# Graph-layer stack: the roots of two quarters on GpSimd, a first stage without side checks, and a fixed order at the start of layer 2

## The chip, the cores and the metric

One core of one Trainium2 chip. The metric is the device time of one execution in microseconds (us), as the median of several runs. The engines are named PE (TensorE; PEld are its weight loads), DVE (VectorE), ACT (ScalarE), POOL (GpSimd) and SP (SyncE, which here only issues DMAs).

## The reference, cut to what matters

Four graph layers stand one behind the other, each as `x = x + layer(relu(layernorm(x)))`, on 4096 nodes of 64 values and a dense 4096 x 4096 adjacency of zeros and ones.

```
# layer 1
adj_att = sigmoid(left[:, None] + right[None, :] + b) * adj
x_local = logmap(x[:, None, :], x[None, :, :], c)       # for every pair of nodes
support = einsum('ij,ijd->id', adj_att, x_local)
out = proj(expmap(x, support, c), c)                    # norms: square roots, one tanh
# layer 2
deg = adj.sum(1) + 1
z = concat([X, (adj @ X + X) / deg]) @ W + b
out = relu(z) / max(norm(relu(z)), 1e-12)
# layer 3
rank = cumsum(adj != 0, axis=1); deg = rank[:, -1:]; k = minimum(deg, 100)
pos = rank - (deg - k)
w = (adj != 0) * where(pos > 0, 0.5 ** (k - pos), 0)
out = w @ (x @ weight) + bias
```

Layer 0 is a graph attention of eight heads with an output attention; the change doesn't touch it.

## The kernel before, in words

**Layer 1, pairs** (`pairs_fast`, L2282, 1188 to 1672 us). The 4096 nodes are 8 groups of 512, and a job is a pair of groups (gi, gj). There are 36: (0,0), (1,1), then the rows gi = 7 down to 2, each with gj = 0 to gi, and last (1,0). A job off the diagonal works both ways: node i's sum over j and node j's over i. The loop over jobs (n from -2 on, L2491) is a software pipeline of depth four: `later` is the job whose distances are worked, `soon` the one that gets its scores, `now` the one whose sums are taken, `done` the one that is closed. Each job has four steps s. In one step the code issues, in this order: the scores (`score_pair`: PE L2331 and L2337 into the two buffers pl, then ACT's sigmoid L2342 into sg), the columns of results (`last_column` and `bring` on DVE, into VT, L2443 to L2451), transposes (`turn`: PE L2387, DVE L2390), sums (PE L2397 into accj and acci), distances (PE L2351 and L2352, ACT L2353) and their squares (ACT L2363), then `end_nodes`, the factor (DVE L2371), checks of the adjacency, and the weighing of the scores (DVE L2378). `in_order` (L933) ties each instruction on PE, DVE and ACT to the one before it on its engine, so those three run in the order in which the code stands. POOL and SP are not tied.

**Ends of nodes.** When a quarter of the nodes (16 blocks of 128) has all its sums, a generator `nodes` (L3051) ends it: `finish_steps` (L2513) turns the sums into the layer's output, `norm_steps` (L994) does layer 2's layernorm, and two copies L3057 and L3064 with a difference hs (L3060) make the two fp16 halves HH of layer 2's input. The pair jobs call it through `end_nodes`: a step of the generator ends at a `yield`, and a yield of True ends the turn. Quarters 24, 16 and 8 (named by their first block) are begun in the pair jobs, as groups 6, 4 and 2 finish; quarter 0, and what is left of 8, is done by the interleaving loop at L2674 to L2680, at the start of layer 2. Each quarter needs three sets of roots of 128 x 8 values: of the norm (un, L2569), of the clip (pp, L2596), of the variance (L1020). Each has two forms, chosen by `beside[0]`: ACT's Sqrt, or `inverse_root` (L981), an estimate on DVE and three Newton rounds of four operations on GpSimd:

```
for _ in range(3):
    nc.gpsimd.tensor_tensor(t, y, y, ALU.mult)
    nc.gpsimd.tensor_tensor(t, t, v, ALU.mult)
    nc.gpsimd.tensor_scalar(t, t, -0.5, 1.5, ALU.mult, ALU.add)
    nc.gpsimd.tensor_tensor(y, y, t, ALU.mult)
```

In this kernel `beside[0]` becomes False at n = -2, before any quarter ends, so all roots are ACT's. Sigmoid and Sqrt are in different function tables of ACT.

**Checks.** All through the kernel the adjacency is read in pieces of 512 KB (`check_rows`, L967: an SP DMA at L964, four pieces ahead, and a pass on DVE, L972) to find values other than 0 and 1. `CHECKS_2` and `CHECKS_3` say how many are left for layers 2 and 3.

**Layer 2** (`layers_fast`, L2622, from 1672). Its weights come by GpSimd DMAs; L2654 works on w2e, and L2660 and L2661 fill sel, the selector for counts. The edges come in eight quarters q = 7 to 0 of 1 MB (tile m2, L2787, three buffers; SP). For each, 16 matmuls sum neighbours (nacc, L2824) and 16 count them (dc, L2834), for the first four groups of targets. hT2 is a transposed copy of the layer's input with a row of ones (a DMA at L2723). Each group's tail (`layer2_group`) then runs beside a segment: `segment(k)` (L2860) does the sums and counts of one of the four other groups of targets, sums at L2870 and counts at L2879, blocks 0 to 31 in rising order. This stage isn't in `in_order`; the framework's scheduler places its instructions.

**Layer 3** (1795 on) ranks the neighbours on PE (L2929, L2937), clamps on ACT and DVE (L2951, L2953) and sums (L2961). The weight squares wsq (L2707) feed its first small matmul pm (L2709).

Of the kernel before, what the change touches and what calls it, by code (L numbers as in the profile page):

```python
# [10 lines left out]
F32 = mybir.dt.float32  # L11
BF16 = mybir.dt.bfloat16
F16 = mybir.dt.float16
F8 = mybir.dt.float8e4
# [3 lines left out]
U8 = mybir.dt.uint8  # L18
# [41 lines left out]
NS = HW // G  # L60
QB = NB // 4
CW = N // 4
CHECKS_2 = 10
CHECKS_3 = 40
HB = NB // 2
EDGE = 56.0
EDGES4 = 0x38383838
# [774 lines left out]
def kernel(  # L842
# [235 lines left out]
    with ExitStack() as l0:  # L1078
# [1203 lines left out]
    def pairs_fast(es, VT, nodes):  # L2282
# [24 lines left out]
        with ExitStack() as ss:  # L2307
# [155 lines left out]

            def end_nodes(s, most):
                while ends and most:
                    if s % 2 == 0 and ends[0][1] < 2:
                        return
                    wait = next(ends[0][0], None)
                    ends[0][1] += 1
                    if wait is None:  # L2470
                        ends.pop(0)
                    most = 0 if wait else most - 1
# [5 lines left out]
            with in_order():  # L2478
                for n in range(-2, len(jobs) + 1):
                    done, now, soon, later = (job(n + k) for k in range(-1, 3))  # L2480
                    if later and n + 2 > 0:
                        load_edges(*later)
                    for s in range(4):
                        if soon and s // 2 < len(ways(*soon)):
                            score_pair(*ways(*soon)[s // 2], s % 2 * 2)
                        if s == 0 and done:
                            last_column(*done, 2)
                            bring(*done)
                        if s % 2 == 0 and now and now[0] != now[1]:
                            turn(*now, s)  # L2490
                        if s % 2 and now:  # L2491
                            sums(*now, s - 1)
                        if s == 2 and now:
                            last_column(*now, 0)
                        if later:
                            distance(*later, s)
                            if s % 2:
                                square(*later, s - 1)
                        busy = bool(ends)
                        beside[0] = beside[0] and bool(soon)  # L2500
                        if now:
                            end_nodes(s, 3 if not soon else 1 + s % 2 * (now[0] < 4) if s else 0)
                        if s == 1 and soon:
                            factor(*soon)
                        if n >= 0 and soon and s % 2 == 0:
                            check_edges(1 if busy else 2 if s or now[0] == now[1] else 1)
                        if s == 3 and soon:
                            weigh(*soon)
                            check_edges(4 if n < 0 else 0)
# [112 lines left out]
    VBITS = 128.0  # L2622


    def layers_fast(es, wide, nodes, ends, parts, ready):
        HO2 = N // 4
        NK = HO2 // G
        HH, SS = parts
# [45 lines left out]
        with in_order():  # L2674
            for quarter, after in zip(ends, ends[1:] + [iter(())]):
                most = 12
                for wait in quarter:
                    for _ in range(min(2, most) if wait else 0):
                        next(after, None)
                        most -= 1  # L2680

# [37 lines left out]
        late, late_x = (lp.tile([P, 2, G], BF16, name=n) for n in ("late", "late_x"))  # L2719

        valued = []
        hT2 = lp.tile([D + 1, N], F32, name="hT2")
        nc.sync.dma_start(hT2[D : D + 1, :], ones[0:NB, :])  # L2723
        for b0 in reversed(range(0, NB, GB)):
            transpose_to(
# [58 lines left out]
            nc.gpsimd.tensor_tensor(xg, xg, b3t.unsqueeze(1).to_broadcast([P, GB, D]), ALU.add)  # L2784

        def rows_of_edges(width):
            m = work.tile([P, JT * HW], U8, name="m2", tag="m2", bufs=3)  # L2787
            return m.rearrange("p (t i) -> p t i", i=width)

        def in_turn(one, other):  # L2790
# [23 lines left out]
        segments = []  # L2814
        accs = [rank_bank("nacc") for _ in range(NS)]
        dc = sum_bank("dc")
        for n, q in enumerate(reversed(range(NQ))):
            m = rows_of_edges(HW)
            nc.sync.dma_start(m, mask_d[q][0])
            m8 = m.bitcast(F8)  # L2820
            for t in range(JT):
                j = q * JT + t
                for k in range(NS):
                    nc.tensor.matmul(  # L2824
                        accs[k],
                        lhsT=HH[:, j].rearrange("p s d -> p (s d)"),
                        rhs=m8[:, t, k * G : (k + 1) * G],
                        start=(n == 0 and t == 0),
                        stop=(n == NQ - 1 and t == JT - 1),
                    )  # L2830
            for t in range(JT):
                j = q * JT + t
                for k in range(NS):
                    nc.tensor.matmul(  # L2834
                        dc[k * O : (k + 1) * O, :],
                        lhsT=sel[:, j * O : (j + 1) * O],
                        rhs=m8[:, t, k * G : (k + 1) * G],
                        start=(n == 0 and t == 0),
                        stop=(n == NQ - 1 and t == JT - 1),
                    )  # L2840
# [17 lines left out]
        in_turn_all(*(layer2_group(g * GB, ev[g], deg[:, g, :]) for g in range(NS)))  # L2858

        def segment(k):  # L2860
            acc, dc = sum_bank("nacc"), rank_bank("dc")
            m8 = [rows_of_edges(G).bitcast(F8) for _ in range(2)]
            for q in range(NQ):
                t = q * JT % HB
                nc.sync.dma_start(
                    m8[q * JT // HB][:, t : t + JT],
                    mask_d[q][1][:, :, k * G : (k + 1) * G].bitcast(F8),
                )
            for j in range(NB):
                nc.tensor.matmul(  # L2870
                    acc,
                    lhsT=HH[:, j].rearrange("p s d -> p (s d)"),
                    rhs=m8[j // HB][:, j % HB],
                    start=(j == 0),
                    stop=(j == NB - 1),
                )
            for j in range(NB):
                r = j % NS
                nc.tensor.matmul(  # L2879
                    dc[r * O : (r + 1) * O, :],  # L2880
                    lhsT=sel[:, j * O : (j + 1) * O],
                    rhs=m8[j // HB][:, j % HB],
                    start=(j < NS),
                    stop=(j >= NB - NS),
                )
            cf = work.tile([P, G], F32, name="cf", tag="cf")
            nc.vector.tensor_copy(cf, dc)
# [134 lines left out]
    with tc.If(general == 0):  # L3022
        with ExitStack() as es:
# [105 lines left out]
```

## Time and profile before

| what | value |
|---|---|
| median of 3 runs | 1965.71 us (1964.72 to 1967.07) |
| the profiled execution | 1964.7 us, span 1963.0 us |
| granted TensorE clock, mean | 0.95 |
| PE busy | 1772.9 us, 90% of the span |
| DVE busy | 1595.1 us, 81% |
| ACT busy | 1436.7 us, 73% |
| POOL busy | 85.5 us, 4%, 126 instructions |
| HBM read and written | 245.37 MB and 49.46 MB |

The span is the time from the first to the last instruction in the trace; the execution's own time has 1.7 us more. A row of the profile such as "L2342 ACT ... sg<-pl,rb" is a line of the code, its engine, what it writes and what it reads. A wait "PE pl L2331 <- ACT sg L2342" means that PE's instruction on line 2331 stood idle until ACT's on line 2342 was done. On ACT the pair stage has these table loads, by the line at which they stand (count, then busy us and mean ns, then idle us before):

```profile
L2342 ACT ACT_TABLE_LOAD x5 | 6.4, 1283 | 0.1
L2569 ACT ACT_TABLE_LOAD x3 | 3.8, 1283 | 0.1
L2596 ACT ACT_TABLE_LOAD x2 | 2.6, 1283 | 0.0
L1020 ACT ACT_TABLE_LOAD x2 | 2.6, 1283 | 0.0
```

### The profile page before, as it was taken

The numbers are of one execution on the slowest core, as the hardware profiler recorded it, in microseconds if no ns is written. First come the engines' busy times: TensorE is split into PE (matmuls) and PEld (weight loads), VectorE is DVE, ScalarE is ACT, GpSimd is POOL, SyncE is SP. The second block draws the span as 40 slices with busy tenths as digits, with TensorE's granted clock in tenths as the row PEclk, the third lists the DMA queues.
The fourth block names the chain that finished last, engine by engine and source line by source line (L and its number), as shares of the span: only waits on it lengthen the run. The fifth ranks groups of instructions, "written<-read, shape, count | busy, mean of one in ns | idle before, by whom it ended". The sixth has DMA issues, their size and how long they took to land.

```text
span 1963.0 us, 44619 instructions
## 1 busy us (share of the span) xinstructions
PE 1772.9 (90%) x19352; PEld 819.6 (42%) x19367; DVE 1595.1 (81%) x2468; ACT 1436.7 (73%) x1477; POOL 85.5 (4%) x126
## 2 busy tenths in 40 slices
PE   5889999999999989998499967999999998899998
PEld 3444444444444445454244442333333332355433
DVE  6769999998779988997768868898888676755687
ACT  3769888899768988996589956777787785323575
POOL 2000100100000000000111100000000000100000
PEclk8899999999999999998699986999999999898999
DMA  8956664425311111102265516455533110664396
GB/s 112 181 126 104 104 99 72 140 104 211 114 50 51 50 50 56 56 2 71 80 186 180 186 54 206 155 177 166 172 108 122 39 33 6 243 210 129 101 338 228
DMA packets 145962, 239.09 MB, mean 122 GB/s; under 512 B 16646, under 2 KB 106070, under 8 KB 140214
## 3 DMA queue, kind: packets, MB, share of 16 engines
q1 hardware_dynamic: 131228, 194.02, 29.7%
q0 software_dynamic: 14528, 42.13, 12.4%
q8 instruction: 153, 2.51, 0.5%
q14 instruction: 53, 0.43, 0.1%
HBM read 245.37 MB, written 49.46 MB: 150 GB/s over the span
## 4 chain that ended last, share of the span: by engine, by line
PE 51%; DVE 20%; ACT 16%; issue 6%; DMA 3%; POOL 0%; SPq 0%; DVEq 0%; ACTq 0%; POOLq 0%
ACT st L1242 9%; PE accj L2397 8%; DVE B L1248 7%; PE accC L1578 6%; PE accB L1578 3%; PE acco L2185 3%; PE pv L2937 3%; DVE st L1236 3%; PE sacc L2961 3%; PE pf L2387 2%; PE pl L2331 2%; PE accD L1578 2%; PE pu L2351 2%; PE pl L2337 2%; PE accL L1578 2%
## 5 line engine op out<-in xcount | busy, mean ns | idle before, releaser
L1242 ACT ACTIVATE st<-srow,nt 128x2048 int8<-128x2048 f32 x352 | 682.9, 1994 | 87.6 <-DVE B L1248 86.4
L1248 DVE TENSOR_TENSOR B<-st,mres 128x1024 int32<-128x1024 int32 x256 | 311.8, 1221 | 63.9 <-PE accC L1578 36.6
L1578 PE MATMUL accB<-B,ybh 128*32 128x512 fp8e4 x3072 | 255.8, 382 | 20.4 <-DVE B L1248 20.2
L1578 PEld LDWEIGHTS <-ybh 128*32 128x32 bf16 (+1 forms) x6656 | 178.5, 97 | 212.3 <-issue 57.0
L1578 PE MATMUL accC<-mres,ych 128*32 128x512 fp8e4 x2272 | 227.3, 380 | 0.0
L1578 PE MATMUL accC<-B,ycn 128*32 128x512 fp8e4 x2272 | 227.1, 379 | 0.0
L1578 PE MATMUL accD<-B,ybh 128*32 128x512 fp8e4 x2048 | 206.6, 382 | 2.1 <-DVE h L1710 2.1
L1236 DVE TENSOR_SCALAR st<-srow,nt 128x2048 uint8<-128x2048 f32 x160 | 205.4, 1285 | 1.8
L2397 PE MATMUL accj<-sg,who 128*64 128x512 f32 (+1 forms) x512 | 199.9, 621 | 7.4 <-DVE sg L2390 6.0
L2397 PE MATMUL acci<-sg,who 128*64 128x512 f32 (+1 forms) x512 | 200.6, 622 | 0.3 <-DVE VT L2451 0.3
L2353 ACT ACTIVATE yt<-pu,consts 128x512 f32<-128x512 f32 x144 | 98.6, 687 | 99.0 <-PE pu L2352 98.8
L2342 ACT ACTIVATE sg<-pl,rb 128x512 f32<-128x512 f32 x256 | 161.0, 679 | 10.9 <-PE pl L2337 8.3
L1578 PEld LDWEIGHTS <-ych 128*32 128x32 f16 x4096 | 117.7, 97 | 116.5 <-issue 12.0
L1578 PE MATMUL accL<-B,ybh 128*32 128x512 fp8e4 x1536 | 156.9, 384 | 4.1 <-DVE h L1709 4.0
L972 DVE SCALAR_TENSOR_TENSOR raw<-raw 128x1024 f32<-128x1024 f32 x128 | 153.9, 1217 | 1.5 <-DMA raw<-in_adj_dram 1.5
L1242 ACT ACTIVATE st<-srowo,nto 128x1024 int8<-128x1024 f32 x128 | 138.1, 1137 | 16.1 <-DVE B L1248 13.7
L1256 DVE TENSOR_TENSOR C<-B,mres 128x1024 int32<-128x1024 int32 x114 | 139.6, 1225 | 3.1
L1578 PE MATMUL accC<-C,ych 128*32 128x512 fp8e4 x1824 | 125.5, 385 | 6.2 <-DVE C L1256 6.1
L2951 ACT ACTIVATE w3b<-pv 128x512 int16<-128x512 f32 x168 | 89.0, 596 | 55.8 <-issue 21.2
L2331 PE MATMUL pl<-nm,noid 128*128 128x512 fp8e4 x256 | 84.2, 394 | 25.5 <-ACT sg L2342 24.4
L1578 PEld LDWEIGHTS <-ycn 128*32 128x32 f16 x2272 | 65.9, 97 | 59.6 <-issue 0.4
L2371 DVE SCALAR_TENSOR_TENSOR yt<-sqy,yt 128x1024 f32<-128x1024 f32 x72 | 84.9, 1219 | 3.4 <-ACT sqy L2363 3.4
(519 smaller groups left out, 2717.6 us busy)
## 6 DMA issues: line engine op xcount, KB each, us to landing
raw<-in_adj_dram SPq DMA_DIRECT2D x128, 512.0 KB, 5.0
mo<-edges SPq DMA_DIRECT2D x32, 512.0 KB, 4.3
noedge<-nmo POOLq DMA_DIRECT2D x32, 512.0 KB, 3.9
nm<-noedge SPq DMA_DIRECT2D x64, 256.0 KB, 3.0
m<-edges SPq DMA_DIRECT2D x32, 512.0 KB, 5.6
srow<-srow_d SPq DMA_DIRECT2D x15, 1024.0 KB, 7.5
mres<-in_adj_dram POOLq DMA_DIRECT2D x8, 1024.0 KB, 36.4
edges<-in_adj_dram POOLq DMA_DIRECT2D x8, 1024.0 KB, 15.0
```

The source lines that it names most:

```text
L972: nc.vector.scalar_tensor_tensor(raw, raw, 0.0, raw, ALU.is_gt, ALU.not_equal, accum_out=bad[:, c : c + 1])
L1236: nc.vector.tensor_scalar(st[:, i, :].bitcast(U8), srow, negs[:, i : i + 1], EDGE, ALU.is_gt, ALU.mult)
L1242: nc.scalar.activation(st[:, i, :], srow, AF.Sign, bias=negs[:, i : i + 1], scale=-1.0)
L1248: nc.vector.tensor_tensor(B.bitcast(I32), st.bitcast(I32), edges.bitcast(I32), ALU.bitwise_and)
L1256: nc.vector.tensor_tensor(C.bitcast(I32), B.bitcast(I32), edges.bitcast(I32), ALU.bitwise_xor)
L1578: ins = nc.tensor.matmul(acc[k * O : (k + 1) * O, :], lhsT=values, rhs=moving(k), start=start, stop=stop,)
L2331: nc.tensor.matmul(pl, lhsT=noid, rhs=nm[:, b, :].bitcast(F8), start=True, stop=False)
L2342: nc.scalar.activation(sg[:, b0 + k, :], pl, AF.Sigmoid, bias=rb[:, j : j + 1], scale=1.0)
L2353: nc.scalar.activation(far[gi, gj][:, b, :], pu, AF.Sigmoid, bias=nb_t, scale=2.0 * DIST_K / (DIST_S * DIST_S),)
L2371: nc.vector.scalar_tensor_tensor(y, squares.pop((gi, gj, b0)), F_K1, y, ALU.add, ALU.mult)
L2397: nc.tensor.matmul(acc[r : r + n, :], lhsT=XQ[:, src, cols], rhs=w, start=start, stop=stop)
L2951: nc.scalar.activation(wk, pvs[i, k], AF.Relu)
```

## The change

1. `CHECKS_2` goes from 10 to 12 and `CHECKS_3` from 40 to 44, and the checks that stood in the first two jobs (n = 0 and 1) are left out; the four ahead of them stay.
2. `beside[0]` is True for all jobs but the last, so the roots of quarters 24 and 16 are made by `inverse_root`; those of 8 and 0 still by ACT. `end_nodes` waits for an odd step only while `beside[0]` is True, and the last job takes up to four steps of ends at a time rather than three.
3. hT2 is no tile of its own: it lies in VT, which is free once the last fold matmuls have read it. m2 has five buffers in place of three.
4. In the loop that ends the last quarters, the next quarter moves one step at each wait rather than two.
5. The main sums of layer 2 are put in program order, two quarters at a time: q = 7, 6 and 5, 4 with sums and counts each; then the counts of 3 and 2, the sums of the first segment over its second half of blocks (16 matmuls), the sums of 3 and 2; then the counts and the sums of 1 and 0. Segments run over falling blocks, their second half first.

GpSimd loads its function library once. In the instruction order of before this stands ahead of L2654; in that of the changed kernel it stands behind L2292, at the start of the pair stage, since the first GpSimd arithmetic now comes there.

```
-CHECKS_2 = 10
-CHECKS_3 = 40
+CHECKS_2 = 12
+CHECKS_3 = 44
...
             def end_nodes(s, most):
                 while ends and most:
-                    if s % 2 == 0 and ends[0][1] < 2:
+                    if beside[0] and s % 2 == 0 and ends[0][1] < 2:
                         return
...
-                        beside[0] = beside[0] and bool(soon)
+                        beside[0] = n < len(jobs) - 1
                         if now:
-                            end_nodes(s, 3 if not soon else 1 + s % 2 * (now[0] < 4) if s else 0)
+                            end_nodes(s, 4 if not soon else 1 + s % 2 * (now[0] < 4) if s else 0)
                         if s == 1 and soon:
                             factor(*soon)
-                        if n >= 0 and soon and s % 2 == 0:
+                        if n > 1 and soon and s % 2 == 0:
                             check_edges(1 if busy else 2 if s or now[0] == now[1] else 1)
...
-                    for _ in range(min(2, most) if wait else 0):
+                    for _ in range(min(1, most) if wait else 0):
...
-        hT2 = lp.tile([D + 1, N], F32, name="hT2")
+        hT2 = VT[0 : D + 1]
...
-            m = work.tile([P, JT * HW], U8, name="m2", tag="m2", bufs=3)
+            m = work.tile([P, JT * HW], U8, name="m2", tag="m2", bufs=5)
...
-        for n, q in enumerate(reversed(range(NQ))):
+        quarters = list(reversed(range(NQ)))
...
+        def segment_sums(k, part):
+            if part:
+                acc = sum_bank("nacc")
+                halves_of[k] = acc, [None, None]
+            acc, m8 = halves_of[k]
+            m8[part] = rows_of_edges(G).bitcast(F8)
+            for q in reversed(range(part * NQ // 2, (part + 1) * NQ // 2)):
+                t = q * JT % HB
+                nc.sync.dma_start(
+                    m8[part][:, t : t + JT],
+                    mask_d[q][1][:, :, k * G : (k + 1) * G].bitcast(F8),
+                )
+            for j in reversed(range(part * HB, (part + 1) * HB)):
+                nc.tensor.matmul(
+                    acc,
+                    lhsT=HH[:, j].rearrange("p s d -> p (s d)"),
+                    rhs=m8[part][:, j % HB],
+                    start=(j == NB - 1),
+                    stop=(j == 0),
+                )
+
+        halves_of = {}
+        with in_order():
+            for n in range(0, NQ, 2):
+                two = [edges_of(q) for q in quarters[n : n + 2]]
+                if n == NQ // 2:
+                    for q, m8 in two:
+                        counts_of(q, m8)
+                    segment_sums(0, 1)
+                    for q, m8 in two:
+                        sums_of(q, m8)
+                elif n > NQ // 2:
+                    for q, m8 in two:
+                        counts_of(q, m8)
+                    for q, m8 in two:
+                        sums_of(q, m8)
+                else:
+                    for q, m8 in two:
+                        sums_of(q, m8)
+                        counts_of(q, m8)
...
         def segment(k):
...
+            if k not in halves_of:
+                segment_sums(k, 1)
+            segment_sums(k, 0)
+            acc, m8 = halves_of.pop(k)
+            dc = rank_bank("dc")
...
-            layers_fast(es, wide, nodes, ends, (HH, SS), ready)
+            layers_fast(es, wide, nodes, ends, (HH, SS), ready, VT)
```

`edges_of` loads a quarter; `sums_of` and `counts_of` hold the two loops of matmuls that stood in the old loop.

More of the change, by code (lines that the diff above doesn't have):

```diff
@@ L2622, with layers_fast @@
     VBITS = 128.0
-    def layers_fast(es, wide, nodes, ends, parts, ready):
+    def layers_fast(es, wide, nodes, ends, parts, ready, VT):
         HO2 = N // 4
@@ L2816, in layers_fast, with edges_of, sums_of @@
         dc = sum_bank("dc")
-        for n, q in enumerate(reversed(range(NQ))):
+        quarters = list(reversed(range(NQ)))
+        def edges_of(q):
             m = rows_of_edges(HW)
             nc.sync.dma_start(m, mask_d[q][0])
-            m8 = m.bitcast(F8)
+            return q, m.bitcast(F8)
+        def sums_of(q, m8):
             for t in range(JT):
@@ L2827, in layers_fast, with counts_of @@
                         rhs=m8[:, t, k * G : (k + 1) * G],
-                        start=(n == 0 and t == 0),
-                        stop=(n == NQ - 1 and t == JT - 1),
+                        start=(j == NB - JT),
+                        stop=(j == JT - 1),
                     )
+        def counts_of(q, m8):
             for t in range(JT):
@@ L2837, in layers_fast @@
                         rhs=m8[:, t, k * G : (k + 1) * G],
-                        start=(n == 0 and t == 0),
-                        stop=(n == NQ - 1 and t == JT - 1),
-                    )
+                        start=(j == NB - JT),
+                        stop=(j == JT - 1),
+                    )
+        def segment_sums(k, part):
[37 more added lines that the diff above has]
+                        counts_of(q, m8)
         cf = work.tile([P, G], F32, name="cf", tag="cf")
@@ L2860, in segment @@
         def segment(k):
[L2861 to L2877, printed above, removed]
+            if k not in halves_of:
[3 more added lines that the diff above has]
+            dc = rank_bank("dc")
+            for j in reversed(range(NB)):
                 r = j % NS
@@ L2882, in segment @@
                     rhs=m8[j // HB][:, j % HB],
-                    start=(j < NS),
-                    stop=(j >= NB - NS),
+                    start=(j >= NB - NS),
+                    stop=(j < NS),
                 )
```

## The prediction

> **What bounds the kernel now.** I read the busy time of each engine by stretch first, then what TensorE (PE) waits for there, then ScalarE's (ACT's) timeline at those waits, and last the start of layer 2. "x" counts instructions, PEclk is the granted TensorE clock.
>
> ```profile
> core 0: us, PE busy (x) PEld busy (x) DVE busy (x) ACT busy (x) POOL busy (x), PEclk, DMA share, GB/s
> 1440.00:1510.00 70.00, 61.88 (x329) 20.74 (x322) 61.74 (x108) 56.65 (x80) 0.00 (x0) 0.98 0.35 109
> 1570.00:1640.00 70.00, 62.98 (x330) 22.14 (x330) 51.81 (x90) 55.58 (x78) 0.00 (x0) 0.95 0.09 27
> 1240.00:1440.00 200.00, 194.60 (x1071) 69.62 (x1070) 173.74 (x235) 149.85 (x212) 0.00 (x0) 0.98 0.52 166
> 1672.00:1690.00 18.00, 10.90 (x47) 4.82 (x46) 15.15 (x51) 5.54 (x11) 3.04 (x7) 0.62 0.63 224
> 1690.00:1728.00 38.00, 38.00 (x258) 16.41 (x257) 20.09 (x58) 9.93 (x19) 0.00 (x0) 0.96 0.79 270
> 1630.00:1640.00 10.00, 9.57 (x42) 2.96 (x43) 4.05 (x7) 6.82 (x12) 0.00 (x0) 0.83 0.00 0
> ```
>
> Where only pairs run (1240 to 1440) PE is busy for 97% and sets the pace. In the two stretches in which a quarter of the nodes ends beside the pairs (rows 2 and 3) it is busy for 88 and 90%, though VectorE (DVE) and ACT have time left: something serial stops it. At 1630 the clock is 0.83. At the start of layer 2 (1672 to 1690) PE works 10.9 of 18 us at 0.62.
>
> PE's waits name the cause. These are the answers for 1440 to 1515, for 1585 to 1640, for 1240 to 1440, and for 1660 to 1820 (us in total, times, longest):
>
> ```profile
> PE pl L2331 <- ACT sg L2342: 8.0, 10, 2.4
> ...
> PE pl L2331 <- ACT sg L2342: 6.0, 9, 2.3
> ...
> PE pl L2331 <- ACT sg L2342: 3.8, 8, 1.2
> ...
> PE dc L2834 <- POOL sel L2661: 6.7, 1, 6.7
> ```
>
> The scores' buffers wait for ACT's sigmoids: 8.0 and 6.0 us in the quarters' stretches, against 3.8 in 200 us of plain pairs. ACT's timeline shows why, and GpSimd's (POOL's) shows the last wait:
>
> ```profile
> 1454.80 1.28 ACT L2569 ACT_TABLE_LOAD   x1
> 1456.10 0.21 ACT L2569 ACTIVATE un<-un 128x8 f32<-128x8 f32 x1
> 1456.32 1.28 ACT L2342 ACT_TABLE_LOAD   x1
> 1457.62 1.27 ACT L2342 ACTIVATE sg<-pl,rb 128x512 f32<-128x512 f32 x2
> ...
> 1686.27 0.86 POOL L2654 TENSOR_SCALAR w2e<-w2e 64x64 f32<-64x64 f32 x2 [12.50 <-issue]
> ...
> 1743.22 0.73 DVE L1023 SCALAR_TENSOR_TENSOR h<-h,ln_var 128x256 f32<-128x256 f32 x1
> 1744.07 0.42 DVE L1023 SCALAR_TENSOR_TENSOR h<-h,ln_var 128x256 f32<-128x256 f32 x1
> ```
>
> A root of eight columns (0.21 us) costs two table loads, and the next scores stand behind them. The chain of waits runs through these loads. In layer 2 the first GpSimd arithmetic (L2654) starts 12.5 us after the instruction before it; the chain has a weight's DMA until 1678.30 and then 7.97 us of "issue". The fill of sel stands behind it, and PE's counts (dc) behind that.
>
> **A. First jobs without checks.** The first two jobs lose 8 checks of 1.22 us on DVE (L972). What PE loses to them is little: it waits 1.2 us (accj for VT L2443) and 0.3 (acci for VT L2451), and works cold behind that (the first acci pair takes 1.94 us where later ones take 1.25, and 1222.7 to 1225.5 runs at half clock, some 1.35 us lost). 1.2 + 0.3 + 0.7 + 1.35 = 3.5 us. Ends: 1 (the waits only move to the first loads of nm) and 6 (the other waits of that stretch, 2.6 for the sigmoids, shrink too). Six of the eight go elsewhere: two to layer 2, four to layer 3 (the constants); costed there.
>
> **B. Roots on GpSimd.** Only the quarters that end beside jobs before the last change, 24 and 16; quarters 8 and 0 keep ACT's roots. By the order of instructions ACT loses 12 loads there: 12 x 1.283 = 15.4 us. PE gets less: its waits in the two stretches, 8.0 + 6.0, minus what row ends cost anyway (3.8 in a stretch with two of them), 10.2 us; and at 1630 to 1640 the clock of 0.83 would be 1.0, 1.7 us. Together 11.9.
>
> The rule: the Trainium skill, "ScalarE: Activation LUTs", section "What ACT_TABLE_LOAD costs", puts a switch at 1283 ns and a drain of about 1380, 2.66 us in all; 12 x 2.66 = 31.9 us would go. In the trace the next activation starts 0.02 us after the load: no drain of that size is left between them. I take the row, 15.4, as the ceiling.
>
> The new work: inverse_root is 12 dependent GpSimd operations of 128x8; with what stands around it the norm (un) has 14, the clip (pp) 12, the layernorm (ln) 13, so 39 for a quarter and 78 in all. None is in this trace. The nearest row, the pair at L2654, takes 0.86 us for two, 0.43 each: un 6.0 us, pp 5.2, ln 5.6. The generator gives them time: two pair jobs' transposes lie 12.84 us apart in the chain, so one of a job's four steps is 3.2; un is asked for after three steps (9.6), pp after two (6.4), ln after three. All fit, pp with 1.2 us to spare. If they don't, ACT's tanh (L2567) or DVE's L2606 or L1023 waits, and behind it, in program order, the next sigmoids on ACT, or on DVE the next copies of transposes and products; PE then stands for the difference. The first GpSimd arithmetic of the stage may pay its start: now it is at 1188, right behind two memsets, and unused for 250 us, so I take +1 for the first operation (0 to +8, the 7.97 of issue above).
>
> The rule against this change: the Trainium skill, "SBUF — State Buffer", section "Who interferes with whom", says GpSimd and DVE share a port pair under an exclusive lock. The rows of L1023 show it: of two equal operations in a row, the one beside GpSimd work takes 0.73 us, the next 0.42. That is 0.31 late (one at 1783.56 reads 0.96, 0.54 late). By the row at its worst the 78 operations put 78 x 0.31 = 24 us, or 78 x 0.54 = 42 us, on DVE. But DVE stood 8.3 + 18.2 = 26.5 us idle in the two stretches, of which 11.9 go if they shrink by that: 14.5 us stay to take it up[...]. I take 0.1 each, 8 us, under the slack, and +1.5 on the path. B: -11.9 + 1 + 1.5 = -9.5 us (ends -13 and -1).
>
> The last job gets four steps of ends rather than three: fold matmuls move ahead of its sums, where PE now waits 1.99 us for a product of DVE. Half of that, 1 us, is in C's sum.
>
> **C. Start of layer 2.** As GpSimd's start is paid at 1188, w2e is worked when its DMA lands: 1678.30 + 0.86 + 0.24 gives sel at 1679.4, before PE asks (1680.8). The wait of 6.7 goes, with the cold work behind it (dc 1.90 for 16 where later ones take 1.05, nacc 5.60 against 3.63: 2.9 us). Not all of it is won. In the fixed order the next matmul that must wait is layer 3's pm (L2709), for wsq on DVE, which stands behind the last quarter's end (hs at 1701.14, LDf's 2.29 us, wsq at 1705.62). The quarters' ends go one at a time instead of two, so this comes no earlier; PE, now 9.6 us ahead, would wait there about 3 us and redo some cold. Main sums end at 1725.2 instead of 1728.0: -2.8. The first segment's half, 16 matmuls, 3.6 us, only moves from behind the groups into the quarters; it fills part of the wait above, and at the end of layer 2 its absence takes 3.1 us off (4.8 us of sums there now, 1.7 then). The stretch between is bound by the groups' chain (PE waits 3.0 us there for ln_var, in three waits), and two more checks (L972) stand in it: +1.2. With the 1 us of the last job the sum is -2.8 - 3.1 + 1.2 - 1 = -5.7; I take -4.5, since the filler helps only if the chain it hides is short. Ends -10 and 0.
>
> **D. At nothing.** Four more checks in layer 3 (DVE 1.22 each, 4.9 us): PE is busy 155.5 of the last 168 us and DVE's clamps share with ACT; uncovered it costs up to 4.9. On SP's queue the ones row now lies in VT and waits for VT's last reader (about 1674.7); the quarters' loads of 1 MB behind it land about 1681, needed from 1686; two more buffers cover that. Uncovered: 3 us.
>
> **Sum.** -3.5 - 9.5 - 4.5 = -17.5. The profiled execution took 1964.7 us (span 1963.0 and 1.7 around it): 1947.2. It lies 1.0 under the median, so 1948. Its own range, half way from each term to its ends: -9.8 to -23.3, 1942 to 1956.
>
> **Rivals.**
> *R1, the waits are replaced.* pp has only 1.2 us to spare; if GpSimd operations take 0.6 us in place, DVE waits at L2606 and the scores wait for products instead of sigmoids; in layer 2 pm takes the place of sel. For it: DVE is busy 61.7 of 70 us in the first stretch. Against: the next GpSimd row is 0.43. Then A -1.5, B -4, C -1: 1965.7 - 6.5 = 1959.
> *R2, slower: the port.* Each of the 78 operations holds DVE up for p; from p = (14.5 + 11.9 + 8) / 78 = 0.44 us the slack, B's gain and the 8 us of A and C are spent. At the highest row, 0.54, it is 42 - 14.5 - 11.9 = 15.7 for B, minus 8: 1973. For it: the rows of L1023, and DVE is nearly full in the first stretch. Against: the second stretch has 18 us of room, and 0.54 was one of the longest delays.
> *R3, nothing comes of it:* PE's time is pairs, and the clock takes back what the waits gave: 1965.
>
> **Chances.** About 0.2% (4 us) is what a measurement of this kernel can tell from no change. Likeliest 0.55, all faster. R1 0.23, of which 0.05 within. R2 0.15, slower. R3 0.07, of which 0.06 within and 0.01 slower. Faster 0.73, same 0.11, slower 0.16. The range reaches from A, B and C all at their best (-6 - 13 - 10: 1937) over R1 to R3 with a little above it, 1967; R2 is left out.
>
> **What would show it.** In the changed profile: no table load on ACT from 1240 to the last job, or B has not happened. PE's wait pl for sg in the quarters' stretches at 4 us rather than 6 to 8. GpSimd rows of 0.3 to 0.45 us start to start, and no wait of DVE L2606 or ACT L2567 for POOL beyond 1 us; if these show 2 us and more, R1. DVE's mean of L2371, L2378 and L972 in those stretches up by 0.1 us at most; up by 0.3, R2. No wait of dc for sel, and instead pm for wsq near 3 us. In the first jobs accj no longer waits for VT. I am wrong if DVE is busy 95% in the quarters' stretches, or if the main sums' end isn't earlier against the last job's end.

## The result, and the profile after

The changed kernel takes 1936.96 us (median of 4 runs, 1936.5 to 1941.29) against 1966.39 for the kernel before on the same chip (4 runs): ratio 0.9855, 95% interval 0.9838 to 0.9872, 29.4 us less. Run once more, on another chip, it gave 1940.08 against 1964.41: 0.9879, 0.9864 to 0.9893, 24.3 us less. The forecast was 17.5 us faster, range 1937 to 1967. The sign is right, the size too small: the first median lies on the range's low edge, where A, B and C were all to come out at their best.

The profiled execution of the changed kernel is the slowest of its first four (1941.29, span 1939.6), 23.4 us shorter than before's. Its busy time by stretch, for the stages shown of before (the first quarter's end, the second's, plain pairs, the start of layer 2 and its main sums):

```profile
core 0: us, PE busy (x) PEld busy (x) DVE busy (x) ACT busy (x) POOL busy (x), PEclk, DMA share, GB/s
1430.00:1500.00 70.00, 67.05 (x360) 22.91 (x358) 64.73 (x111) 52.31 (x76) 12.32 (x26) 0.98 0.39 121
1555.00:1620.00 65.00, 61.51 (x340) 22.51 (x342) 51.80 (x88) 48.31 (x71) 11.18 (x27) 1.00 0.11 33
1240.00:1430.00 190.00, 184.65 (x1018) 66.00 (x1016) 166.30 (x225) 142.97 (x203) 0.00 (x0) 0.99 0.52 167
1653.00:1670.00 17.00, 16.33 (x104) 6.45 (x104) 13.99 (x43) 4.73 (x9) 3.38 (x6) 0.91 1.00 366
1670.00:1706.00 36.00, 31.03 (x212) 15.59 (x210) 19.90 (x57) 9.30 (x17) 0.61 (x1) 0.95 0.77 248
```

PE now works 96 and 95% of the quarters' stretches, close to the 97% of plain pairs. At the start of layer 2 it works 16.3 of 17 us, but the main sums behind it, which were without a gap, have one of 5 us. The waits, for 1430 to 1500, 1555 to 1622, 1645 to 1775 (PE) and 1420 to 1640 (DVE), say the same:

```profile
PE pl L2331 <- ACT sg L2342: 1.9, 4, 1.2
...
PE pl L2331 <- ACT sg L2342: 2.1, 5, 1.2
...
PE pm L2709 <- DVE wsq L2707: 5.0, 1, 5.0
...
PE dc L2840 <- POOL sel L2661: 0.3, 1, 0.3
...
DVE mden L2606 <- POOL pp_root L991: 2.7, 2, 1.5
```

8.0 and 6.0 us of waiting for sigmoids became 1.9 and 2.1; no table load is left on ACT from 1240 to 1645, where quarter 8's begin. sel's 6.7 became 0.3, and pm's wait for wsq stands in its place. DVE waits for GpSimd's clip root twice (1.2 and 1.5 us), and PE doesn't feel it. GpSimd's timeline at the first root, from its second operation on:

```profile
1451.06 1.06 POOL L989 TENSOR_TENSOR un_roott<-un_roott,un 128x8 f32<-128x8 f32 x1
1452.22 1.05 POOL L990 TENSOR_SCALAR un_roott<-un_roott 128x8 f32<-128x8 f32 x1
1453.35 0.20 POOL L991 TENSOR_TENSOR un_root<-un_root,un_roott 128x8 f32<-128x8 f32 x1
1453.63 0.20 POOL L988 TENSOR_TENSOR un_roott<-un_root 128x8 f32<-128x8 f32 x1
1453.91 0.20 POOL L989 TENSOR_TENSOR un_roott<-un_roott,un 128x8 f32<-128x8 f32 x1
```

Of the 78 operations 57 take 0.20 to 0.26 us (0.28 start to start). The other 21 take 1.03 to 1.20, and each of them stands beside L2371, L2378 or L972: VectorE instructions of 1.22 us whose two inputs both lie in SBUF, the on-chip memory that the engines share. Beside L2390 and L2445, one of whose inputs is a PSUM buffer (PE's results), no operation is held up. VectorE loses nothing (L2371 from 1240 to 1640: mean 1219 ns before, 1218 now).

**Where the time went.** Landmarks read from the timelines: the first square (L2363), the last sum of pairs (L2397), plate (the small matmul that follows the main sums), the first pv of layer 3. "Slow" is the number of clock windows of 3.41 us at half speed within the pair stage from 1210 us on (all profiles begin the stage at half speed), or the half-speed time in the others; the clock's fall in the last 6 us of layer 3 is left out.

| | before | changed | changed, second profile |
|---|---|---|---|
| pairs, us (slow windows) | 478.7 (8) | 456.4 (2) | 458.9 (4) |
| pairs' end to main sums' end, us | 60.8 | 56.5 | 57.0 |
| groups' tails, us (slow us) | 65.4 (10.2) | 66.1 (13.7) | 59.8 (0) |
| layer 3, us (slow us) | 168.1 (0) | 168.1 (0) | 168.1 (0) |

The first changed profile enters the pairs 2.4 us later than before's, in code that is the same; 2.4 - 22.3 - 4.3 + 0.6 + 0.1 = -23.4 (rounded at each step). Most of the gain is in the pairs, and six slow windows fewer are part of it.

**The clock.** Job by job, from square to square, 20 of the 35 intervals agree within 0.05 us in both kernels. Most of the others lie in the first jobs and beside the ends of quarters. Job (6,1) doesn't: it takes 14.14 us before and 12.59 after, though the change does nothing there. The windows view cut at the clock's own edges, before first, then the changed kernel:

```profile
1321.27:1324.69 3.42, 1.98 (x8) 0.50 (x9) 3.42 (x6) 3.21 (x5) 0.00 (x0) 1.00 0.75 274
1324.69:1328.10 3.41, 3.41 (x14) 0.57 (x11) 2.05 (x2) 2.19 (x4) 0.00 (x0) 0.50 0.75 246
```

```profile
1318.21:1321.62 3.41, 2.02 (x9) 0.40 (x8) 3.41 (x6) 3.21 (x6) 0.00 (x0) 1.00 0.60 226
1321.62:1325.03 3.41, 3.41 (x25) 1.57 (x24) 2.40 (x4) 3.09 (x5) 0.00 (x0) 1.00 0.96 305
1403.54:1406.95 3.41, 2.00 (x9) 0.54 (x8) 3.41 (x5) 3.09 (x6) 0.00 (x0) 1.00 0.99 320
1406.95:1410.37 3.42, 3.40 (x9) 0.56 (x9) 3.17 (x4) 1.82 (x3) 0.00 (x0) 0.50 0.56 183
```

The same wait of 1.24 us (pl for sg, behind a diagonal job) occurs in all three. In the two windows in which PE is busy 1.98 and 2.00 us, the next runs at half speed; where the wait falls so that it is 2.02, it doesn't. Counted over the pair stages of all fourteen profiles, of 59 full-speed windows with PE busy for 2.00 us or less, 47 are followed by one at half speed; of about 1700 with more, 2 are. So this is no exact rule. Two windows of the changed kernel, each with the one behind it, go the other way:

```profile
1635.65:1639.06 3.41, 1.75 (x16) 0.86 (x8) 2.48 (x4) 0.03 (x1) 0.00 (x0) 1.00 0.00 0
1639.06:1642.47 3.41, 3.08 (x22) 2.35 (x24) 2.31 (x5) 0.00 (x0) 0.00 (x0) 1.00 0.00 0
1741.46:1744.87 3.41, 3.41 (x26) 2.65 (x25) 1.03 (x4) 1.49 (x5) 0.00 (x0) 1.00 0.46 153
1744.88:1748.29 3.41, 3.41 (x15) 2.26 (x14) 1.91 (x5) 0.59 (x1) 0.00 (x0) 0.50 0.38 100
```

The second pair lies in the groups' tails. What else the clock follows is open. Its changes in each trace lie on a grid of 3.4133 us whose place differs from run to run. That agrees with the Trainium skill, "TensorE: Matmul & The Clock Gate", Part 1, on a free-running window of 3413 ns. The page has the clock fall after an idle window; here one that was 58% busy was enough, and the measurement decides. A slow window in the pairs costs about 1.5 us (14.14 - 12.59 = 1.55).

### The profile page after: what moved, and what is told of

It is laid out like the page before. It is cut to its first block, busy times and chain, and to the rows that moved or that the text cites. A ratio compares the mean times of both kernels' runs of the same rounds, so it can differ in the third digit from the quotient of the medians.

```text
span 1939.6 us, 44688 instructions
## 1 busy us (share of the span) xinstructions
PE 1762.3 (91%) x19352; PEld 821.1 (42%) x19367; DVE 1592.7 (82%) x2462; ACT 1422.4 (73%) x1463; POOL 120.4 (6%) x204
## 4 chain that ended last, share of the span: by engine, by line
PE 51%; DVE 22%; ACT 15%; issue 6%; DMA 2%; POOL 0%; SPq 0%; DVEq 0%; ACTq 0%
ACT st L1242 9%; PE accj L2397 8%; DVE B L1248 7%; PE accC L1578 6%; PE accB L1578 3%; PE acco L2185 3%; PE pv L2973 3%; DVE st L1236 3%; PE sacc L2997 3%; PE pf L2387 2%; PE pl L2331 2%; PE accD L1578 2%; PE pu L2351 2%; PE pl L2337 2%; PE accL L1578 2%
## 5 line engine op out<-in xcount | busy, mean ns | idle before, releaser
L2397 PE MATMUL accj<-sg,who 128*64 128x512 f32 (+1 forms) x512 | 195.6, 611 | 5.6 <-DVE sg L2390 5.4
L2397 PE MATMUL acci<-sg,who 128*64 128x512 f32 (+1 forms) x512 | 195.6, 611 | 0.0
L2342 ACT ACTIVATE sg<-pl,rb 128x512 f32<-128x512 f32 x256 | 160.9, 679 | 10.2 <-PE pl L2337 7.6
L1578 PEld LDWEIGHTS <-ych 128*32 128x32 f16 x4096 | 117.8, 98 | 116.9 <-issue 12.6
L972 DVE SCALAR_TENSOR_TENSOR raw<-raw 128x1024 f32<-128x1024 f32 x128 | 153.9, 1216 | 0.0
L1256 DVE TENSOR_TENSOR C<-B,mres 128x1024 int32<-128x1024 int32 x114 | 139.5, 1225 | 3.1
L2371 DVE SCALAR_TENSOR_TENSOR yt<-sqy,yt 128x1024 f32<-128x1024 f32 x72 | 84.8, 1218 | 3.4 <-ACT sqy L2363 3.4
```

What stands on the lines that cost most here:

```text
L972: nc.vector.scalar_tensor_tensor(raw, raw, 0.0, raw, ALU.is_gt, ALU.not_equal, accum_out=bad[:, c : c + 1])
L1256: nc.vector.tensor_tensor(C.bitcast(I32), B.bitcast(I32), edges.bitcast(I32), ALU.bitwise_xor)
L1578: ins = nc.tensor.matmul(acc[k * O : (k + 1) * O, :], lhsT=values, rhs=moving(k), start=start, stop=stop,)
L2342: nc.scalar.activation(sg[:, b0 + k, :], pl, AF.Sigmoid, bias=rb[:, j : j + 1], scale=1.0)
L2371: nc.vector.scalar_tensor_tensor(y, squares.pop((gi, gj, b0)), F_K1, y, ALU.add, ALU.mult)
L2397: nc.tensor.matmul(acc[r : r + n, :], lhsT=XQ[:, src, cols], rhs=w, start=start, stop=stop)
```

## The experiments

The first four kernels shared a chip (before: 1965.78, 43 runs from 1957.19 to 1973.83), the next four another (1966.79, 15 runs), the last four a third (1964.41, 12 runs). Each ratio is to the kernel before on the same chip, and ratios, not medians, are compared between chips.

**1. Roots back on ScalarE** (from the changed kernel; one early GpSimd operation keeps the library's load early; the edit is shortened)

```
-                        beside[0] = n < len(jobs) - 1
+                        beside[0] = False
+                        turns[0] = n < len(jobs) - 1      # end_nodes asks turns[0]
```

> The changed kernel with the roots of quarters 24 and 16 back on ScalarE; one early GpSimd operation keeps the library's load at the start of the pair stage, everything else is as changed. Theory (the roots' twelve table loads and the stalls behind them are worth about 12 us): the median goes from 1937 to 1949, PE's wait of pl for sg in the quarters' stretches rises by 8 to 10 us. Prediction's term: 9.5 us, 1946.5. Rival (the roots hardly matter, the gain came from the clock's windows falling elsewhere): under 1941.

Measured: 1958.95, ratio 0.9970 (0.9959 to 0.9980). Pairs 472.6 us with 6 slow windows. The old waits are back, here for 1440 to 1515 and 1560 to 1640 (2.1 and 4.0 us in the changed kernel):

```profile
PE pl L2334 <- ACT sg L2345: 8.2, 11, 2.4
...
PE pl L2334 <- ACT sg L2345: 6.2, 10, 2.3
```

The rival falls; by the ratios (0.9970 against 0.9855 and 0.9879) the roots are worth 18 to 23 us, more than the 9.5 of the prediction and the 12 of the theory. In the pairs they are 472.6 - 456.4 = 16.2 us: four windows more at 1.45 are 5.8, and 10.4 are the waits. This profile also has 13.7 us of slow clock in layer 3 (173.5 us instead of 168.1).

**2. Checks back in the first two jobs**

```
-                        if n > 1 and soon and s % 2 == 0:
+                        if n >= 0 and soon and s % 2 == 0:
```

> The changed kernel with the checks back in the first two jobs. Theory: the trace puts 6 us on this part, half of it half-speed clock windows, so 1943, with accj waiting for VT again in the first jobs. Prediction's term: 3.5 us, 1940.5. Rival (the checks cost nothing there, the gain at that place came from the clock alone): 1937 to 1938.

Measured: 1950.51, 0.9929 (0.9904 to 0.9954). The wait is back, from 1205 to 1240:

```profile
PE accj L2397 <- DVE VT L2443: 2.0, 1, 2.0
```

Pairs 463.1 us, 6.7 more than in the first changed profile. Both this run and the changed kernel have 72 checks in the pair stage, so it has 7 more in the first jobs and 7 fewer later. Windows slowed in the first jobs are back (2 of the 4 in this profile); 6.7 - 2 x 1.45 = 3.8 is the wait and what follows from it. The rival falls. The median is further up than 1943; this profile, too, has 13.7 us of slow clock in layer 3.

**3. Start of layer 2 in the scheduler's order**

```
-        with in_order():
-            for n in range(0, NQ, 2):
...
+        for q in quarters:
+            q, m8 = edges_of(q)
+            sums_of(q, m8)
+            counts_of(q, m8)
...
-                    for _ in range(min(1, most) if wait else 0):
+                    for _ in range(min(2, most) if wait else 0):
```

> The changed kernel with the main sums of layer 2 in the scheduler's order, no segment sums between them, and two steps of interleaving. The library is still loaded early. Theory (the order and the early half are worth little beside the early library): 1937 to 1939. Prediction: of its 5.7 us some 3 are the early half, so 1940. Rival (the fixed order carries the whole of the 3.7 us seen there): 1941.

Measured: 1943.05, 0.9894 (0.9868 to 0.9920), which can't be told from the changed kernel's 0.9879 (0.9864 to 0.9893). Main sums end 54.6 us after the pairs rather than 56.5, since the half segment (3.6 us) isn't among them; the tails take 65.7 us with 10.2 of slow clock, and layer 3 172.1 us with 10.2. The fixed order and the early half carry nothing that shows. The rival falls.

**4. The library early, alone** (from the kernel before)

```
+        early = fp.tile([P, 8], F32, name="early")
+        nc.gpsimd.memset(early, 1.0)
+        nc.gpsimd.tensor_tensor(early, early, early, ALU.mult)
```

> The kernel before with a single early GpSimd operation, so that its library is loaded at the start of the pair stage. Theory: dc no longer waits 6.7 us for sel, but the next wait (wsq, or the ends of the last quarter) takes most of it: 2 to 4 us faster, 1962 to 1964. Rival 1 (the wait was on the path in full, with the cold work behind it): 9 us, 1957. Rival 2 (all of it is taken back): 1966.

Measured: 1965.32, 1.0000 (0.9988 to 1.0013). PE's waits at the start of layer 2:

```profile
PE pm L2712 <- DVE wsq L2710: 7.2, 1, 7.2
```

The wait for sel is gone, and pm waits 7.2 us for wsq instead. Main sums end 60.4 us after the pairs, as before (60.8). Rival 2 is right: the 6.7 us were off the path, hidden by the last quarter's end on DVE. (What moves here is one of four: each trace has GpSimd's MODIFY_POOL_CONFIG at four places, before at 1.9, 16.3, 1673.8 and 1815.7 us, and the third moves to 1190.9 in the changed kernel. "Once" holds for that one alone.)

**5. Roots on GpSimd, alone** (from the kernel before)

```
-                        beside[0] = beside[0] and bool(soon)
+                        beside[0] = n < len(jobs) - 1
```

> The kernel before with the roots of quarters 24 and 16 on GpSimd and nothing else (the library's load comes early with it). Theory: 12 us for the roots and 2 to 4 for the library, 1951. Prediction's terms: 9.5 and about 3, 1953.5. Rival (the roots pay only with the first jobs unchecked or with the last job's new rule): 1957 or above.

Measured: 1958.0, 0.9950 (0.9931 to 0.9969), 8.8 us, less than expected. But the profile's pairs are 461.9 us with 4 slow windows, 16.8 less than before's: 5.8 for four windows fewer, 11.0 for the waits. Some of it is lost behind the pairs: main sums end 62.2 us after them, 1.4 later than before, and this profile has 13.7 us of slow clock in layer 3 (173.3 us). By the median alone the rival (1957 or above) would stand; by the stage it falls. How often layer 3 begins slow, one profile can't tell.

**6. PE kept busy behind diagonal jobs** (from the kernel before)

```
+            def keep_busy(count):
+                pf = ps_f.tile([P, G], F32, name="pf", tag="pf")
+                for _ in range(count):
+                    nc.tensor.matmul(pf, lhsT=LC[:, 0:P], rhs=XC[:, 0:G], start=True, stop=True)
...
+                            if s == 2 and now and now[0] == now[1] and n > 1:
+                                keep_busy(5)
```

> The kernel before with five matmuls that nobody reads in step 2 of each diagonal job but the first two, 1.1 us of PE's work in the place where it waits 1.24 us for the sigmoids. Clock theory: windows of 3.41 us in which PE stands too long are followed by one at half speed, at 1.5 us each; the trace of before has four behind these waits (1324.7, 1413.4, 1560.2, 1614.8). They go: 4 to 6 us faster, 1961. Rival (the windows are chance or follow something else): the same four windows stay, and the time is 1966 or up to 2 us more.

Measured: 1959.82, 0.9956 (0.9936 to 0.9977). PE's timeline at job (6,1):

```profile
1325.53 1.24 PE L2364 MATMUL pf<-XAf,LDf 128*128 128x512 f16 x5
1326.92 0.38 PE L2331 MATMUL pl<-nm,noid 128*128 128x512 fp8e4 x1 [0.15 <-ACT sg L2342]
1327.50 0.38 PE L2331 MATMUL pl<-nm,noid 128*128 128x512 fp8e4 x1 [0.20 <-ACT sg L2342]
```

Five useless matmuls stand where PE waited, the job takes 12.59 us, and the four windows behind diagonal jobs are gone; those in the first jobs and at the table loads stay. Pairs 473.1 us, 5.6 less. Work that nobody reads made the kernel about 7 us faster. The clock theory holds as far as these four windows go, and its rival falls.

**7. GpSimd loaded beside VectorE**: 96 multiplications of 128 x 8 (from the changed kernel)

```
+                        if 4 <= n < 10:
+                            for _ in range(4):
+                                nc.gpsimd.tensor_tensor(early, early, early, ALU.mult)
```

> The changed kernel with 96 more GpSimd operations of 128 x 8 that nobody reads, four in each step of six plain pair jobs. Theory (the shared port makes GpSimd wait, not VectorE): 1937, VectorE's operations there as long as before, GpSimd's at 0.2 us alone and about 1.05 beside VectorE. Rival (the slower case of the prediction: each delays VectorE by 0.3 to 0.54 us): 29 to 52 us more on VectorE against some 10 us of slack in these jobs, so 1955 to 1979.

Measured: 1942.1, 0.9885 (0.9860 to 0.9910). Nothing tied the operations to their steps: GpSimd ran all from 1199.9 to 1249.7, right behind its library's load (8.13 us without work). That stretch, here and in the changed kernel:

```profile
1200.00:1250.00 50.00, 46.40 (x215) 14.21 (x214) 40.09 (x52) 39.55 (x57) 42.18 (x96) 0.89 0.48 160
```

```profile
1200.00:1250.00 50.00, 46.14 (x220) 14.08 (x222) 40.76 (x52) 39.98 (x58) 0.00 (x0) 0.91 0.50 156
```

VectorE is busy 40.1 us here and 40.8 there, for 52 instructions each; from 1225 to 1300 its checks read 1216 ns against 1215. GpSimd's operations took from 194 to 1283 ns. GpSimd waits, VectorE doesn't: rival 2 of the prediction has no price to pay. By its time the run can't be told from the changed kernel (0.9879); its pairs are 459.1 us with 4 slow windows.

**8. Squares of layer 3's weights on GpSimd** (from the changed kernel)

```
-            nc.vector.tensor_tensor(wsq, w3, w3, ALU.mult)     # inside not_before_nodes
+        nc.gpsimd.tensor_tensor(wsq, w3, w3, ALU.mult)         # ahead of it
```

> The changed kernel with the squares of layer 3's weights on GpSimd, ahead of the wait for the last quarter. Theory: pm no longer waits 5.0 us for wsq, PE waits for the last quarter's h and hs instead, some 1.5 us: 3.5 us faster, 1933.5. Rival (the last quarter's end sets the time there anyway): 1936 to 1937.

Measured: 1942.71, 0.9890 (0.9864 to 0.9916): no gain. PE's waits from 1645 to 1735:

```profile
PE pm L2709 <- POOL wsq L2686: 3.7, 1, 3.7
PE tr L1037 <- DVE h L1023: 3.4, 2, 1.9
```

The scheduler put pm far ahead, where it waited 3.7 us, and the transposes (tr) then waited 3.4 us for the last quarter's h (1.5 in the changed kernel). Main sums end 57.5 us after the pairs. The rival holds: taking one wait away from PE's queue brings the next.

**9. The changed kernel again**

> The changed kernel once more, unedited, as the mark for the others on the same chip. The kernel before spread from 1957 to 1974 us over 43 runs, and so far the changed one has four runs. Clock theory (the free-running windows of the TensorE clock fall differently in each execution): its runs spread over 10 us or more too, with a median of 1939 to 1942, and the profile has half-speed windows in other places than the first one. Rival (the first four are typical): 1936.5 to 1938, spread under 5 us.

Measured: 1940.08 (1936.79 to 1940.68), 0.9879. The median is what the clock theory said, the spread of these four runs (3.9 us) is not. The windows differ in part: the two behind diagonal jobs are in both profiles, two in the last job are new (4 in the pairs), and the groups' tails have none (59.8 us; 66.1 in the first profile). So the profile supports the theory where the spread doesn't.

**10. The filler in the changed kernel** (the edit of 6)

> The changed kernel with five matmuls that nobody reads in step 2 of each diagonal job but the first two. Clock theory: the windows behind the diagonal jobs (1407 and 1485 in the first profile of the changed kernel) are gone, 2 to 4 us faster than the changed kernel on this chip. Rival: no change or up to 2 us slower.

Measured: 1937.94 (1936.63 to 1943.09), 0.9875 (0.9859 to 0.9890). No slow window from 1210 to the pairs' end, and pairs of 453.4 us, the shortest so far; by the time alone it can't be told from run 9.

**11. pm and the transposes behind the main sums** (from the changed kernel: the blocks from wsq to fold_3 and of `transpose_to` move behind the main sums' `in_order`, nothing else)

```
+        for b0 in reversed(range(0, NB, GB)):
+            transpose_to(...)
+        wsq = lp.tile([D, D], F32, name="wsq3")
...
         cf = work.tile([P, G], F32, name="cf", tag="cf")
```

> The changed kernel with two blocks issued behind the main sums of layer 2: the weight squares with their matmul pm, and the transposes of the layer's input. Theory (PE's queue is in order: what stands behind pm waits for the last quarter's end, so pm's place sets the loss, not the wait for sel): the 5.0 us wait of pm for wsq goes, all sums of quarters 7 to 2 and the counts of 1 and 0 stand ahead of the last quarter's end, and the time is 4 to 6 us below the changed kernel on this chip. Rival (the transposes and the scaled weights become late for the groups' tails instead): same time or slower.

Measured: 1941.95, 0.9891 (0.9877 to 0.9905): no faster. The wait of 5.0 is gone and the main sums end 53.6 us after the pairs, 3 less, as the theory has it; but the tails had 10.2 us of slow clock and took 64.5. At full clock that is about 59.9 (0.45 us for each slow us, see C below), as in run 9, so the late transposes of the rival don't show either. The time doesn't show a gain, so as a gain the theory isn't shown.

**12. Both edits** (10 and 11)

> Both edits at once: the filler in the diagonal jobs and the two blocks behind the main sums. Theory: the gains add, 6 to 9 us below the changed kernel on this chip. Rival (the clock's windows give back what is won): no better than the better of the two.

Measured: 1938.63 (1935.21 to 1946.96), 0.9873 (0.9855 to 0.9892). Pairs 453.3 and main sums 53.5 us, each as in its own run; but 13.7 us of slow clock in the tails and as much in layer 3 (174.7 us). The theory's gain of 6 to 9 us doesn't come: no version beats the changed kernel by more than can be told.

## Why the prediction was right or wrong

The direction and the main mechanisms held. The forecast came out too small chiefly because the clock's slow windows, named in the terms A and B only in passing, were no term of their own.

**A, first jobs (3.5 forecast).** Right in kind, too small. Run 2 puts it at 6.7 us in the pairs. The prediction counted one half-speed stretch (1.35 us, 1222.7 to 1225.5) and cold work behind the waits (0.7); two whole windows lie there, 2 x 1.45, and 3.8 us are the rest.

**B, roots (9.5 forecast).** The mechanism and its main term hold. The waits were to give 10.2 us; run 1 shows 10.4 and run 5 11.0. The row of the table load (no drain behind it) stands; 31.9 us were never there. Two terms of the sum failed, +1 for the first GpSimd operation and +1.5 for the port. The first root began with an operation of 1.03 us and was done at 1458.2, 2 us before ACT's tanh (1460.4). The 0.43 us for an operation came out by luck: GpSimd is busy 34.2 us for the 78, 0.44 each, but this is a mix of 0.20 and 1.05, so the first un took 8.3 us rather than 6.0 and the first pp 6.0 rather than 5.2. The price of the port came from rows where VectorE's L1023 stood beside long GpSimd work: a cast of 128x512 (0.61 us) for the delay of 0.31, an addition of 128x256 (0.73 us) for that of 0.54. In both L1023 ends 0.27 to 0.28 us after GpSimd does. Beside operations of 0.20 us nothing reached VectorE, and GpSimd paid. The Trainium skill, "SBUF — State Buffer", section "Who interferes with whom", says that a VectorE instruction with two SBUF inputs contends with a GpSimd one that reads SBUF, and that the order of issue decides who blocks. The traces agree: the 21 slow operations all stand beside such instructions. As an estimate from the durations, GpSimd then waits for up to 1.2 us, and VectorE for 0.2 at most. The step "78 x 0.31" took the delay as one per operation, where it goes by the other's length.

**The clock, the term that was missing.** I gave it 1.7 us at 1630 and about 2 in A. Take 1.45 us a window, an estimate from profiles that differ in little else (453.4, 456.4 and 458.9 us of pairs with 0, 2 and 4 windows, so 1.25 to 1.5) and from the 1.55 above. Then pairs without slow windows are 467.1 us in the kernel before (478.7 - 8 x 1.45), 467.3 in run 6, 456.1 in run 5, 457.3 in run 2, 463.9 in run 1, and 453.1 to 453.6 in all profiles with roots and checks as changed. So 13.6 us are waits, of the kind that A and B counted, and 4 to 6 windows fewer are another 6 to 9. Two each of the eight belonged to A and B; the other four stood behind diagonal jobs that no edit touches. Two of that kind are left in each changed profile; the second one has two more in the last job, behind a wait of 1.98 us. How many of the other four go is the grid's chance.

**C, start of layer 2 (4.5 forecast).** The sum is near by luck (4.3 us in the main sums; the tails, compared at equal clock by 0.45 us for each us at half speed, as the 59.8 and 66.1 us give it, about 1.0 us), and its steps are wrong. "The wait of 6.7 goes" for a net of 2.8 was the first step; run 4 shows that this alone is worth nothing. The early half gives about 1 us in the tails, not 3.1 (run 3: 61.1 at equal clock, 59.9 with it), for 1.9 more in the main sums; the fixed order gives nothing that shows. The 1 us of the last job didn't come: PE still waits 1.98 us for the same product, now at the fold matmuls (L2532), and from the transposes ahead of that wait to the last sum the stage takes 12.6 us instead of 12.0; behind it, pvt waits 1.7 instead of 2.6. The wait of pm was foreseen at 3 us and is 5.0. What did shorten the main sums is argued from the order of instructions, no run shows it alone: pm sits at a fixed place in PE's order and comes up 36 to 39 us after the pairs' end in all kernels with the library early and pm and wsq in their old places (37.2 in run 4, 37.8 in the changed kernel), as DVE sets it. In run 4 the order has 143 matmuls of sums and counts ahead of it, in run 3 172, in the changed kernel 190 (in run 3 DVE is done with wsq 1.7 us earlier, so pm waits 2.9 us there). Run 11 fits: with pm behind all of them the sums end 2.9 us earlier. Work that stands ahead of the wait is done while DVE sets the time. Which edit lets the scheduler place more there (five buffers, hT2 in VT, the last job's rule) was not separated and stays open.

**D** held: layer 3 took 168.1 us in both, and the queue of SP delayed a first quarter by 0.4 us.

**Rivals.** R1's waits came (L2606 1.2 and 1.5 us, over the 1 us of the forecast and under the 2 of R1; pm 5.0), but only pm's reached PE. DVE is busy 92% of the first quarter's stretch, under the 95% that would have been a sign of being wrong. R2 is excluded by run 7. R3 said that the clock would take back what the waits gave: it did the reverse, since the profiles with fewer waits have fewer slow windows (8 before, 6 in run 1, 4 in runs 2 and 5, 2 and 4 as changed).

**What stays open.** The groups' tails and layer 3's start also have slow stretches, 0 to 13.7 us: the tails in 11 of the 14 profiles, layer 3 in 7. Each kernel but the changed one has one profile, so how much of a median's distance comes from there isn't known: run 2's and run 1's medians lie 10 and 19 us over run 9's, on other chips, where their pairs account for 4 and 14. And the changed kernel's first profile is its slowest run, 4.3 us over its median; where the faster runs gain that, no trace shows.

## What to carry to other kernels

When PE sets the pace, cost a wait of a microsecond or two twice: its own length (1.2 us here), and the chance that it slows the next window of the clock (1.5 us here). Before a wait is counted as gain, remove it alone and see which instruction waits in its place. When two engines contend, ask how long the other's instruction is: here many short operations beside long ones cost the long ones nothing that could be seen.

## What the runs showed of the hardware that was not expected

- The clock changes on a grid of 3.4133 us. In the pair stages, a window in which PE was busy for 2.00 us or less was followed by one at half speed in 47 cases of 59, one with more in 2 of about 1700; in the groups' tails one that was busy throughout was followed by half speed too. The kernel before spread over 17 us in 43 runs (1957 to 1974), and the windows are a likely part of that, which single profiles don't show.
- Five matmuls that nobody reads, put into a wait behind each diagonal job, made the kernel before 0.44% faster (0.23 to 0.64).
- GpSimd operations of 128 x 8 take 0.20 us alone and 1.03 to 1.20 beside VectorE instructions with two SBUF inputs, whose own time stayed at 1.22 us.
